# Transposing the last four tiles' attention weights on TensorE, other places for five weights, and one-column Newton steps in the norms

## The chip, the core and the metric

The kernel runs as one program on one core of a Trainium2 chip. Its time is the device time of one execution in microseconds (us); the figure given for a kernel is the median of several executions. The profile comes from one further execution, whose own time is given beside it. The engines are named as the profile names them: PE (TensorE's matmuls, with PEld for its weight loads), DVE (VectorE), ACT (ScalarE), POOL (GpSimd) and SP (SyncE, which here only issues DMA transfers).

## The reference: what is computed

Two layers of a small perceiver-like network on `x` of 32 x 64 x 256 (2048 tokens of 256 numbers), with a context of 32 x 256 x 256. All is float32. Each sublayer adds its result to `x`:

```
x += cross_attention_0(ctx, layernorm(x))    # 16 heads of 64; keys and values from ctx and from the latents
x += linear_attention(layernorm(x))          # 16 heads of 16, relu features
x += gated_ffn(layernorm(x))                 # hidden 768
x += cross_attention_1(layernorm(x), ctx)    # 16 heads of 16, a mask over the 256 keys
x += slstm(layernorm(x))                     # a scan over the 64 positions
x += moe(layernorm(x))                       # 8 experts 256 -> 1024 -> 256, gates by entmax over the 8 logits
```

What matters here is the second cross attention: for each batch item and head, `softmax(q k^T / 4 + mask)` over 256 keys, times `v`; and the layer norm, `(x - mean) / sqrt(var + eps)`.

## The kernel before

**Tiles.** The 2048 tokens are 16 tiles of 128 rows, and a tile holds two batch items. All 16 tiles of `x` stay in SBUF. Everything else lies in one large SBUF array, the arena, in which each named buffer has fixed places (`ar.put(phase, tag, size, *at)`, lines 693 to 756). Places of different phases may overlap; a buffer of a later phase may be written once all users of the overlapping earlier buffers are done. The big weights of the first cross attention are W0 (0 to 2048, the query weights), W1 (2048 to 4096, the transposed key weights), W2 (4096 to 6144, the value weights) and W3 (6144 to 8192). W0 and W1 are last read by the queries of the last group of items, W2 and W3 by the projection of the last tile. PSUM is handled as eight banks.

**Stages.** (1) The first cross attention, item by item (32 items). (2) Per group `g` of two tiles: linear attention, feed-forward, then for each tile the second cross attention, then the sLSTM and the router's logits. (3) The experts, part A for tiles 0 to 11 and part B for tiles 12 to 15, with gathers and scatters by indirect DMA on POOL's queue.

**Who sets the order.** The program is written as calls on `Plan`, which records operations with a `rank` (how early the author wants them) and a `lane` (PE operations of one lane stay in order). `Plan.run` (line 308) then simulates the engines with assumed durations (`PlanEngine.length`, line 519) and issues, again and again, the operation that can start first; an operation whose rank lies more than 12 above the lowest rank left waits (`pl.run(12.0)`, line 1959). For an `either` or a `copy` it picks ACT or DVE, whichever can start first. A transfer's end comes from one shared `wire` of 380 bytes per ns and a latency (lines 359 to 361). `Plan.locks` (line 370) keeps a DVE operation with three inner operands, such as `tensor_tensor` or `scalar_tensor_tensor`, from starting while a POOL operation runs in the plan, and the other way round; a `tensor_scalar` of fewer than 64 elements per row isn't kept so. What comes out is a fixed program: each engine runs its own list in order. All instructions of the plan therefore carry line 420 in the profile, and are told apart by the names of their tiles.

**The norms.** `ln_stats` (line 592) takes mean and variance of `n` tiles at once (n = 4 for the context, n = 2 elsewhere), forms `ve = var + eps`, lets POOL compute `r = ve ** -0.5`, and improves `r` by one Newton step in three DVE instructions on columns of `[128, n]` (lines 612 to 614). `normed` (line 1149) adds one for the shift `nmr = -mean * r`, and applies the norm on ACT or DVE. Both are called per group for `la`, `ff`, `xa`, `sl` and `me`; `lay` (the norm inside linear attention) uses the statistics alone, and so does `norm` (line 801) with a shift of its own for the first layer's `x` and context.

**The second cross attention.** `keys_values(t)` (line 1339) loads the tile's transposed context (`ctxT`), and makes keys (tiles `xak` in PSUM) with `x_wk` and values (`xav`) with `x_wv`. `scores(t, c, q, kT)` (line 1368) handles a block: one tile `t` and one half `c` of the heads, so 32 blocks in all. It computes the scores (`xsc`) into four banks, adds the mask and takes the maximum on DVE, and exponentiates on ACT into `pr`, for the tile's two items `b2`. The weights have then to be transposed so that keys lie on partitions. DVE's `transpose` does that only inside squares of 32 x 32, so that it takes two steps: one stream transpose of 128 x 1024 per item into `bT`, and then sixteen moves that shift pieces of 32 x 512 between partitions into `pT`:

```
for n in range(4):
    for a in range(4):
        k = (a + n) % 4
        move(n, pT[32 * k ...], bT[32 * a ...], tight=True)   # n == 1: a copy on ACT; else a DMA issued by SP
```

So a block has 4 copies on ACT and 12 DMA transfers of 64 KB on SP. `bT` and `pT` have one place each. `weighted` (line 1421) multiplies with `v` (`xpo`), scales by the sums (`xrT`), and `projected` (line 1448) adds the result to `x` (`xpw`).

**Loads.** The second layer's weights are loaded on SP's queue from line 1085 on: the feed-forward weights, then `x_wk`, `x_wv`, `x_wq`, `s_w`, the mask, `x_wo` in 16 pieces, `s_wp` and `m_wr`. Each of them goes out when its place is free. In the kernel before, `x_wk` and `x_wv` lie in W2 (4608 and 5120), `s_w` in W0 (1536), `s_wp` and `m_wr` in W1 (3584, 3840).

Of the kernel before, what the change touches and what calls it, by code (L numbers as in the profile page):

```python
# [9 lines left out]
F32 = mybir.dt.float32  # L10
I32 = mybir.dt.int32
AF = mybir.ActivationFunctionType
ALU = mybir.AluOpType
# [204 lines left out]
class Plan:  # L218
# [89 lines left out]
    def run(self, ahead):  # L308
        free = dict.fromkeys(self.ENGINES, 0.0)
        busy = dict.fromkeys(self.ENGINES, 0.0)  # L310
        wire = 0.0
        hold = {"DVE": (0.0, 0.0), "POOL": (0.0, 0.0)}
        calls_lock = self.locks
        ready = [op for op in self.ops if op.left == 0]
        todo = len(self.ops)
        waiting = set(self.ops)
        rest = sorted(self.ops, key=lambda op: -op.rank)
        while todo:
            best, short = None, None
            while rest[-1] not in waiting:  # L320
                rest.pop()
            for op in sorted(ready, key=lambda op: op.rank):
                if short is not None and op.rank > short.rank and "PE" in op.ways and op.news:
                    continue
                if op.rank > rest[-1].rank + ahead:
                    continue
                at = 0.0
                if op.news and not self.has_room(op):
                    if "PE" in op.ways and (short is None or op.rank < short.rank) and self.has_room(op, True):
                        short = op  # L330
                    continue
                since = self.since(op)
                for engine, (length, _) in op.ways.items():
                    at = max(free[engine], since)
                    for other in op.before:
                        at = max(at, other.done + (0.03 if other.on == engine else self.HOP))
                    for t_ in op.uses:
                        at = max(at, t_.free_at)
                    if engine in hold:
                        (lo, hi), other = hold[engine], calls_lock(op.ways[engine][1][0], engine)  # L340
                        if other and lo <= at < hi:
                            at = hi
                    key = at + (self.lean if engine == "DVE" and len(op.ways) > 1 else 0.0), op.rank
                    if best is None or key < best[0]:
                        best = key, op, engine
            assert best is not None, "nothing can start"
            (at, _), op, engine = best
            length, calls = op.ways[engine]
            todo -= 1
            ready.remove(op)  # L350
            waiting.remove(op)
            op.on = engine
            op.end = op.done = at + length
            free[engine] = op.end - self.OVERLAP.get(engine, 0.0)
            busy[engine] += length
            if engine in hold and self.locks(calls[0], engine):
                hold["POOL" if engine == "DVE" else "DVE"] = at, op.end
            if "dma" in calls[0][0]:
                size = PlanEngine.size_of(calls[0])
                wire = max(wire, op.end) + size / 380e3  # L360
                op.done = max(wire, op.end + size / 220e3) + (2.4 if engine == "POOL" else 1.5)
            self.issue(op, engine, calls)
            for other in op.after:
                other.left -= 1
                if other.left == 0:
                    ready.append(other)
        self.now, self.busy = max(op.done for op in self.ops), busy
# [178 lines left out]
def kernel(ctx: ExitStack, tc: tile.TileContext, d: dict, out: bass.AP):  # L546
# [45 lines left out]
    def ln_stats(srcs, name, lane="", twice=False, nc=nc, small=small):  # L592

        n = len(srcs)
        st = small.tile([P, n, 6], F32, tag=f"st{n}{lane}", name=f"st_{name}")
        mv = small.tile([P, n, 2], F32, tag=f"mv{n}{lane}", name=f"mv_{name}")
        for i, s_ in enumerate(srcs):  # L600
            nc.vector.bn_stats(st[:, i, :], s_)
            nc.vector.bn_aggr(mv[:, i, :], st[:, i, :])
        ve = small.tile([P, n], F32, tag=f"ve{n}{lane}", name=f"ve_{name}")
        if twice:
            nc.vector.tensor_scalar(ve, mv[:, :, 1], 1.0 + EPS, EPS * EPS, ALU.mult, ALU.add)
        else:
            nc.vector.tensor_scalar(ve, mv[:, :, 1], EPS, None, ALU.add)
        r = small.tile([P, n], F32, tag=f"r{n}{lane}", name=f"r_{name}")
        nc.gpsimd.tensor_tensor(r, ve, mhalf[:, 0:n], ALU.pow)

        t_ = small.tile([P, n], F32, tag=f"t{n}{lane}", name=f"t_{name}")
        nc.vector.tensor_tensor(t_, r, ve, ALU.mult)
        nc.vector.scalar_tensor_tensor(t_, t_, -0.5, r, ALU.mult, ALU.mult)
        nc.vector.scalar_tensor_tensor(r, t_, 1.5, r, ALU.add, ALU.mult)
        return mv, r


# [59 lines left out]
    with ExitStack() as sa:  # L677
# [31 lines left out]
        ar.put(1, "oT", 1024, 41472)  # L709

        for tag, size, *at in (
            ("f_wg", 1536, 0), ("s_w", 512, 1536), ("f_wu", 1536, 2048), ("s_wp", 256, 3584), ("m_wr", 16, 3840),
            ("x_wq", 512, 4096), ("x_wk", 512, 4608), ("x_wv", 512, 5120), ("x_wo", 512, 5632), ("f_wd", 1536, 6144),
            ("xTa", 512, 42496, 43008), ("qT", 512, 9728, 43520), ("xn0a", 256, 10240), ("xn1a", 256, 10496),
            ("lak", 256, 10752, 11008), ("kvb0", 272, 11264, 11536), ("kvb1", 272, 11808, 12080), ("y0", 256, 12352),
            ("lav", 258, 14336, 14594), ("y1", 256, 14852),
            ("xn0f", 256, 12800), ("xn1f", 256, 13056), ("xTf", 512, 13312, 13824),
            ("ffh", 1536, 17920), ("sg", 512, 20992, 21504),
            ("xn0x", 256, 16384), ("xn1x", 256, 16640), ("xTx", 512, 16896, 17408), ("xq", 1024, 32256, 33280),
            ("xcT", 1024, 22016, 19456), ("xkT", 1024, 23040, 24064), ("xv", 1024, 30208, 31232),  # L720
            ("xpr", 1024, 25088, 26112, 27136), ("xbT", 2048, 28160), ("xpT", 2048, 35328), ("xne", 256, 37376, 37632, 37888),
            ("xra", 256, 38144, 38400), ("xrT", 256, 38656, 38912), ("mi", 256, 39168), ("xom", 256, 39424, 39680),
            ("xoT", 256, 39936, 40192), ("mb", 256, 40448), ("vd", 256, 40704),
            ("xn0s", 256, 15360, 15616), ("xn1s", 256, 15872, 16128), ("xTs", 512, 34304, 34816),
            ("g_il", 260, 40960), ("g_m", 130, 7680), ("g_fs", 130, 7810), ("g_iz", 130, 7940), ("g_c", 130, 41220),
            ("hsel", 32, 41350), ("vb", 2, 41382), ("bo2", 1, 41384), ("hb", 4, 41386), ("g_z", 128, 12608), ("g_o", 128, 15108),
            ("g_tmp", 128, 41472), ("g_tmp2", 128, 41600), ("g_h", 128, 41728),
            ("a_wq", 512, 8192), ("a_wkv", 1024, 8704), ("rows_a", 1024, 44032),
        ):
            ar.put(2, tag, size, *at)  # L730
# [418 lines left out]
        def normed(srcs, name, lane, twice=False):  # L1149

            mv, r = stats(srcs, name, lane, twice)
            nmr = sp.tile([P, len(srcs)], F32, tag=f"nmr{lane}", name=f"nmr_{name}")
            pl.vector.scalar_tensor_tensor(nmr, mv[:, :, 0], -1.0, r, ALU.mult, ALU.mult)
            xn = []
            for i, s_ in enumerate(srcs):
                n_ = ar.tile([P, D], F32, tag=f"xn{i}{lane}", name=f"xn_{name}_{i}")
# [182 lines left out]
        def keys_values(t):  # L1339
# [25 lines left out]
                pl.copy(v[:, b2], pv)  # L1365
            return kT, v

        def scores(t, c, q, kT):


            pl.lane = "sc"
# [4 lines left out]
            with pl.together(1.45):  # L1376
                for b2 in range(2):
                    for j in range(4):
# [6 lines left out]
                            stop=True,  # L1385
                            tile_position=(32 * j, 0),
                        )
            bT = ar.tile([P, 4, 2, 2, 4, B_], F32, tag="xbT", name=f"xbT{nm}")
            for b2 in range(2):
                pr = ar.tile([P, 4, S2], F32, tag="xpr", name=f"xpr{nm}_{b2}")  # L1390
                for j in range(4):
# [1 line left out]
                    nmax = sp.tile([P, 1], F32, tag="xnm", name=f"xnm{nm}_{j}_{b2}")  # L1393
                    pl.vector.tensor_tensor_reduce(ne, scs[j][:, b2, :], mb, 1.0, 3.0e38, ALU.add, ALU.min, nmax)
                    pl.scalar.activation(pr[:, j, :], ne, AF.Exp, bias=nmax, scale=-1.0, accum_out=sm[:, b2, j : j + 1])
                pl.vector.transpose(
                    bT[:, :, b2].rearrange("p k d j c -> p j d k c"),
                    pr.rearrange("p j (d k c) -> p j d k c", d=2, c=B_),
                )
            pT = ar.tile([P, 4, 2, 2, 4, B_], F32, tag="xpT", name=f"xpT{nm}")  # L1400
            for n in range(4):
                for a in range(4):
                    k = (a + n) % 4
                    move(
                        n,
                        pT[B_ * k : B_ * k + B_, a].rearrange("p b d j c -> p (b d j c)"),
                        bT[B_ * a : B_ * a + B_, k].rearrange("p b d j c -> p (b d j c)"),
                        tight=True,
                    )
# [620 lines left out]
```

## Time and profile before

| what | us |
|---|---|
| three runs, median (lowest to highest) | 1606.68 (1605.44 to 1611.94) |
| the profiled execution's own time | 1614.4 |
| its span, first to last instruction | 1612.7 |
| PE busy, and its idle time between matmuls | 1513.3, some 80 |
| DVE, ACT, POOL busy | 1055.5, 830.6, 481.6 |

The mean granted clock of TensorE over the span is 0.976. The profile's page gives busy time by engine, then rows of 40 slices of 40 us in which a digit is the busy share in tenths. A line of a timeline reads: start, length, engine, operation, written tile <- read tiles, shape, count, and in brackets how long the engine stood idle before it and what released it. A line of a group gives total busy time, the mean in ns, and the idle time of the engine before them. The first layer fills the span to about 865 us, the groups of two tiles follow until about 1440, and the experts' matmuls run from 1376 to the last one at 1599.

### The profile page before, as it was taken

The numbers are of one execution on the slowest core, as the hardware profiler recorded it, in microseconds if no ns is written. First come the engines' busy times: TensorE is split into PE (matmuls) and PEld (weight loads), VectorE is DVE, ScalarE is ACT, GpSimd is POOL, SyncE is SP. The second block draws the span as 40 slices with busy tenths as digits, with TensorE's granted clock in tenths as the row PEclk, the third lists the DMA queues.
The fourth block names the chain that finished last, engine by engine and source line by source line (L and its number), as shares of the span: only waits on it lengthen the run. The fifth ranks groups of instructions, "written<-read, shape, count | busy, mean of one in ns | idle before, by whom it ended". The sixth has DMA issues, their size and how long they took to land. (4 is left out here: it accounts for less than half of the span.)

```text
span 1612.7 us, 25931 instructions
## 1 busy us (share of the span) xinstructions
PE 1513.3 (94%) x8594; PEld 1050.5 (65%) x8594; DVE 1055.5 (65%) x3119; ACT 830.6 (52%) x2193; POOL 481.6 (30%) x740
## 2 busy tenths in 40 slices
PE   7999999999999999999979999999999887899986
PEld 5565656566665656666546666667666665688875
DVE  7667566675665767766564787798897777553130
ACT  5555455454654546545431366666665576632332
POOL 6233224241242313432320122232232122233342
PEclk9999999999999999999999999999999997899998
DMA  5112212121111312123021032333333334655391
GB/s 178 33 33 57 46 26 58 23 60 34 36 40 37 76 30 40 30 73 89 17 60 49 25 78 71 80 85 73 78 88 91 100 85 121 181 151 144 76 301 31
DMA packets 114039, 120.21 MB, mean 75 GB/s; under 512 B 15472, under 2 KB 92081, under 8 KB 113905
## 3 DMA queue, kind: packets, MB, share of 16 engines
q1 hardware_dynamic: 108384, 110.60, 26.4%
q0 software_dynamic: 5520, 7.94, 2.5%
q8 instruction: 69, 1.13, 0.3%
q14 instruction: 66, 0.53, 0.1%
HBM read 63.63 MB, written 7.47 MB: 44 GB/s over the span
## 5 line engine op out<-in xcount | busy, mean ns | idle before, releaser
L420 PE MATMUL pu<-arena 128*128 128x512 f32 (+1 forms) x768 | 305.1, 615 | 7.4 <-DMA arena<-arena 7.4
L420 ACT COPY arena<-arena 32x128 f32<-32x128 f32 (+2 forms) x537 | 247.0, 460 | 118.2 <-DVE arena L420 59.0
L420 PE MATMUL sc<-arena 128*128 128x320 f32 x1024 | 293.0, 434 | 1.0 <-ACT arena L420 0.9
L420 POOL COPY arena<-arena 32x128 f32<-32x128 f32 (+2 forms) x285 | 138.5, 489 | 421.1 <-PE sc L420 264.7
L420 PEld LDWEIGHTS sc<-arena 128*128 128x128 f32 x1024 | 193.3, 190 | 102.3 <-issue 33.0
L420 ACT ACTIVATE arena<-sc,nmax 128x320 f32<-128x320 f32 x256 | 134.2, 526 | 224.0 <-DVE nmax L420 217.3
L420 DVE TENSOR_REDUCE nmax<-sc 128x1 f32<-128x320 f32 x256 | 122.6, 484 | 167.4 <-PE sc L420 164.9
L420 DVE STREAM_TRANSPOSE arena<-arena 128x256 f32<-128x256 f32 (+2 forms) x318 | 206.6, 688 | 26.4 <-POOL arena L420 16.0
L420 PEld LDWEIGHTS pu<-arena 128*128 128x128 f32 (+1 forms) x768 | 114.4, 189 | 158.1 <-issue 146.4
L420 POOL TENSOR_TENSOR arena<-arena 128x512 f32<-128x512 f32 (+2 forms) x157 | 145.3, 945 | 206.9 <-DVE arena L420 192.0
L420 ACT ACTIVATE arena<-arena,xnm 128x256 f32<-128x256 f32 x256 | 127.0, 497 | 41.5 <-DVE xnm L420 40.5
L420 DVE CUSTOM_DVE_ANT_0 arena<-xsc,arena 128x256 f32<-128x256 f32 x256 | 100.0, 417 | 8.2 <-ACT arena L420 6.2
L420 DVE TENSOR_TENSOR arena<-arena,sm 128x1280 f32<-128x1280 f32 x64 | 97.2, 1519 | 1.7
L420 POOL DMA_INDIRECT out<-arena x25 | 39.9, 1596 | 107.0 <-DVE arena L420 72.7
L420 PEld LDWEIGHTS po<-arena 128*64 128x64 f32 x1024 | 55.3, 137 | 21.2 <-issue 12.1
L420 PE MATMUL po<-arena 128*64 128x128 f32 x1024 | 62.7, 276 | 5.3 <-DVE arena L420 3.3
L420 PE MATMUL xav<-arena 128*128 128x256 f32 x256 | 63.1, 392 | 0.0
L420 DVE COPY arena<-pu 128x512 f32<-128x512 f32 x65 | 44.6, 687 | 27.4 <-PE pu L420 26.8
L420 PE MATMUL xak<-arena 128*128 128x512 f32 x128 | 62.3, 613 | 0.0
L420 PE MATMUL mepha<-arena 128*128 128x256 f32 x256 | 60.5, 388 | 0.7 <-ACT arena L420 0.7
L420 PE MATMUL pqk<-arena 64*128 64x256 f32 x512 | 61.1, 381 | 0.0
L420 PE MATMUL pq<-arena 128*128 128x256 f32 x256 | 57.3, 382 | 2.0 <-DVE arena L420 1.3
(396 smaller groups left out, 2510.5 us busy)
## 6 DMA issues: line engine op xcount, KB each, us to landing
arena<-in_m_w SPq DMA_DIRECT2D x26, 1024.0 KB
arena<-arena SPq DMA_DIRECT2D x384, 64.0 KB
arena<-arena SPq DMA_DIRECT2D x256, 80.0 KB
arena<-in_ctx SPq DMA_DIRECT2D x32, 256.0 KB
arena<-in_ctxT SPq DMA_DIRECT2D x16, 512.0 KB
x<-in_x SPq DMA_DIRECT2D x16, 128.0 KB
arena<-in_l0x_wkv SPq DMA_DIRECT2D x2, 1024.0 KB
arena<-arena SPq DMA_DIRECT2D x16, 128.0 KB
```

The source lines that it names most:

```text
L420: r = getattr(real, name)(*[get(a) for a in args], **{k: get(a) for k, a in kw.items()})
```

## The change

Four edits.

1. In `scores`, tiles 12 to 15 (`by_pe`) no longer use `bT` and the moves. Each item's weights are transposed by TensorE in two groups of four 128 x 128 transposes, each group into one PSUM bank, and each bank is copied by ACT or DVE into `pT`. Per block that is 16 transposes and 4 copies of 128 x 512 in place of 2 stream transposes, 4 ACT copies and 12 DMA transfers.
2. In the arena, `x_wk` moves to W0 (1536) and `x_wv` to W1 (3584); `s_w`, `s_wp` and `m_wr` move into W2 (4608, 5120, 5376).
3. In `ln_stats` with n <= 2, the three Newton instructions on both columns become two scalings of a single column by per-partition scalars, one instruction with two constants on both columns, and two more one-column scalings. In `normed`, the shift becomes one instruction per column. The sums are the same: `t = ve * r * r`, `t = 1.5 - t / 2`, `r = r * t`.
4. In the plan's simulation, the wire is kept per issuing engine and at 260 bytes per ns.

```diff
-        wire = 0.0
+        wire = dict.fromkeys(self.ENGINES, 0.0)
...
-                wire = max(wire, op.end) + size / 380e3
-                op.done = max(wire, op.end + size / 220e3) + (2.4 if engine == "POOL" else 1.5)
+                wire[engine] = max(wire[engine], op.end) + size / 260e3
+                op.done = max(wire[engine], op.end + size / 220e3) + (2.4 if engine == "POOL" else 1.5)
...
-        nc.vector.tensor_tensor(t_, r, ve, ALU.mult)
-        nc.vector.scalar_tensor_tensor(t_, t_, -0.5, r, ALU.mult, ALU.mult)
-        nc.vector.scalar_tensor_tensor(r, t_, 1.5, r, ALU.add, ALU.mult)
+        if n <= 2:
+            for i in range(n):
+                nc.vector.tensor_scalar(t_[:, i : i + 1], ve[:, i : i + 1], r[:, i : i + 1], r[:, i : i + 1], ALU.mult, ALU.mult)
+            nc.vector.tensor_scalar(t_, t_, -0.5, 1.5, ALU.mult, ALU.add)
+            for i in range(n):
+                nc.vector.tensor_scalar(r[:, i : i + 1], r[:, i : i + 1], t_[:, i : i + 1], None, ALU.mult)
+        else:
...
-            ("f_wg", 1536, 0), ("s_w", 512, 1536), ("f_wu", 1536, 2048), ("s_wp", 256, 3584), ("m_wr", 16, 3840),
-            ("x_wq", 512, 4096), ("x_wk", 512, 4608), ("x_wv", 512, 5120), ("x_wo", 512, 5632), ("f_wd", 1536, 6144),
+            ("f_wg", 1536, 0), ("x_wk", 512, 1536), ("f_wu", 1536, 2048), ("x_wv", 512, 3584),
+            ("x_wq", 512, 4096), ("s_w", 512, 4608), ("s_wp", 256, 5120), ("m_wr", 16, 5376), ("x_wo", 512, 5632), ("f_wd", 1536, 6144),
...
-            pl.vector.scalar_tensor_tensor(nmr, mv[:, :, 0], -1.0, r, ALU.mult, ALU.mult)
+            for i in range(len(srcs)):
+                pl.vector.tensor_scalar(nmr[:, i : i + 1], mv[:, i, 0:1], r[:, i : i + 1], -1.0, ALU.mult, ALU.mult)
...
+        def by_pe(t, c):
+            return t >= 12
...
+                if by_pe(t, c):
+                    pl.lane = "tp"
+                    if b2 == 0:
+                        pT = ar.tile([P, 4, 2, 2, 4, B_], F32, tag="xpT", name=f"xpT{nm}")
+                    for kc in range(2):
+                        pT_ps = bank([P, 4, P], f"xpTp{nm}_{b2}_{kc}")
+                        with pl.together(T4):
+                            for j in range(4):
+                                tr(pT_ps[:, j, :], pr[:, j, kc * P : (kc + 1) * P], ident)
+                        pl.copy(
+                            pT[:, :, b2, kc].rearrange("p a j c -> p j a c"),
+                            pT_ps.rearrange("p j (a c) -> p j a c", a=4),
+                        )
+                else:
+                    pl.vector.transpose(...)
...
-            for n in range(4):
+            for n in range(0 if by_pe(t, c) else 4):
```

More of the change, by code (lines that the diff above doesn't have):

```diff
@@ L611, in ln_stats @@
         t_ = small.tile([P, n], F32, tag=f"t{n}{lane}", name=f"t_{name}")
-        nc.vector.tensor_tensor(t_, r, ve, ALU.mult)
-        nc.vector.scalar_tensor_tensor(t_, t_, -0.5, r, ALU.mult, ALU.mult)
-        nc.vector.scalar_tensor_tensor(r, t_, 1.5, r, ALU.add, ALU.mult)
+        if n <= 2:
[5 more added lines that the diff above has]
+        else:
+            nc.vector.tensor_tensor(t_, r, ve, ALU.mult)
+            nc.vector.scalar_tensor_tensor(t_, t_, -0.5, r, ALU.mult, ALU.mult)
+            nc.vector.scalar_tensor_tensor(r, t_, 1.5, r, ALU.add, ALU.mult)
         return mv, r
@@ L1387, in scores @@
                         )
-            bT = ar.tile([P, 4, 2, 2, 4, B_], F32, tag="xbT", name=f"xbT{nm}")
+            if not by_pe(t, c):
+                bT = ar.tile([P, 4, 2, 2, 4, B_], F32, tag="xbT", name=f"xbT{nm}")
             for b2 in range(2):
@@ L1395, in scores @@
                     pl.scalar.activation(pr[:, j, :], ne, AF.Exp, bias=nmax, scale=-1.0, accum_out=sm[:, b2, j : j + 1])
[L1396 to L1400, printed above, removed]
-            for n in range(4):
+                if by_pe(t, c):
[12 more added lines that the diff above has]
+                else:
+                    pl.vector.transpose(
+                        bT[:, :, b2].rearrange("p k d j c -> p j d k c"),
+                        pr.rearrange("p j (d k c) -> p j d k c", d=2, c=B_),
+                    )
+            if not by_pe(t, c):
+                pT = ar.tile([P, 4, 2, 2, 4, B_], F32, tag="xpT", name=f"xpT{nm}")
+            for n in range(0 if by_pe(t, c) else 4):
                 for a in range(4):
```

## The prediction

> **What bounds the kernel.** I read the page first, then busy time by stage, then the timelines of TensorE and of the SP queue, because the chain of waits ends on the last indirect write and holds nothing else (two pieces, 1.3 us).
>
> ```profile
> PE 1513.3 (94%) x8594; PEld 1050.5 (65%) x8594; DVE 1055.5 (65%) x3119; ACT 830.6 (52%) x2193; POOL 481.6 (30%) x740
> ...
> PE   7999999999999999999979999999999887899986
> ...
> PEclk9999999999999999999999999999999997899998
> ```
>
> TensorE is busy nearly everywhere; its row dips in two places, at the slices around 840 us and from 1300 us on, and the second dip is also where the granted clock falls. The same by stage (us, then busy us of PE, PEld, DVE, ACT, POOL, then the clock):
>
> ```profile
> 780.00:880.00 100.00, 87.27 (x413) 54.09 (x412) 52.20 (x128) 30.89 (x73) 16.44 (x35) 0.93 0.21 51
> 880.00:1220.00 340.00, 323.61 (x2327) 232.52 (x2325) 281.09 (x997) 202.74 (x554) 86.91 (x164) 0.99 0.28 71
> 1220.00:1410.00 190.00, 161.07 (x1202) 121.14 (x1203) 137.35 (x508) 118.86 (x324) 46.38 (x82) 0.90 0.43 118
> 1410.00:1600.00 190.00, 183.29 (x1058) 159.94 (x1056) 62.37 (x310) 60.16 (x152) 68.80 (x62) 0.98 0.53 149
> ```
>
> What can be won: 12.7 us of TensorE idle at the change of layers, 16.4 in the steady second layer (95% busy), 28.9 in its tail, 6.7 among the experts. In the tail a clock of 0.90 means 38 us at half speed (0.10 x 190 / 0.5), of which TensorE worked 161/190, 32 us, so up to 16 us more. Everything else is TensorE work, and the change adds to that.
>
> **Part 1, the weights' places.** The timeline of TensorE at the change of layers:
>
> ```profile
> 839.80 1.49 PE L420 MATMUL lac<-arena 128*64 128x136 f32 x8 [3.35 <-DVE arena L420]
> 846.12 5.22 PE L420 MATMUL pu<-arena 128*128 128x512 f32 x8 [4.83 <-DMA arena<-arena]
> ...
> 892.13 3.70 PE L420 MATMUL xak<-arena 128*128 128x512 f32 x8
> 895.67 1.89 PE L420 MATMUL xav<-arena 128*128 128x256 f32 x8
> 897.40 0.60 PE L420 MATMUL tr_xa<-ident,arena 128*128 128x128 f32 x4
> 897.83 1.89 PE L420 MATMUL xav<-arena 128*128 128x256 f32 x8
> ```
>
> TensorE stands 3.35 + 4.83 = 8.2 us while the last item's probabilities are transposed and moved, and has nothing else it may do. Keys and values of tile 0 (xak, xav) have their context already (the two ctxT loads issue at 823.01), but not their weights:
>
> ```profile
> 741.12 0.49 SPq L420 DMA_DIRECT2D arena<-in_f_wu  x1
> ...
> 864.64 0.38 SPq L420 DMA_DIRECT2D arena<-in_x_wk  x1
> ...
> 1383.63 9.23 SPq L420 DMA_DIRECT2D arena<-arena  x12
> ```
>
> x_wk and x_wv lie in W2 and wait for its last reader, the projection that ends at 865; in W0 and W1 they can load by 741, as f_wu does. So xak (892.13 to 895.67, 3.5 us) and two xav groups (1.7 each, 3.5) can fall into the hole: their ranks are 40.9 to 42.1, and the planner, which lets a step run 12 ahead of the lowest rank left, allows 41.8 to 43 while item 31's last steps (29.8 to 31) stand. The output of xak lies over score operands that the last scores (834) free; that of xav over a buffer that the last stream transpose (839.6) frees, so xak fits the first gap and xav the second. The copies go to ACT, busy 2.2 of these 10 us. **Bounds: nothing** (planned elsewhere) **to 10.5 us** (both gaps, and half of the 4.6 us worked at half clock there). I take **-7.0**, tile 0's keys and values. The two loads pass 1.4 us of SP issue ahead of the context loads of tile 15 at 742.7, which are wanted tens of us later; s_w, s_wp and m_wr move behind 865, next to x_wo, and are first read over 100 us later. Cost nothing.
>
> **Part 2, the norms.** 56 statistics of two columns go from 3 DVE instructions to 5, and 40 shifts from 1 to 2: 56 x 2 + 40 = 152 more. An undisturbed chain now starts its steps 0.2 us apart (t_ff at 853.52, 853.71, 853.90, nmr at 854.10): 0.8 us. The nearest new form is the pair of 128x2 scalings by a column at 860.57: 0.35 us for two, 0.39 with the same hand-over of 0.04. Three pairs and one plain step are 3 x 0.39 + 0.20 = 1.37, so +0.57 a chain, and without the shift +0.38: 40 x 0.57 + 16 x 0.38 = 29 us of DVE. What goes:
>
> ```profile
> L420 DVE TENSOR_TENSOR t_me<-r_me,ve_me x8: 109/679/683, 999.8 to 1436.1; 128x2 f32<-128x2 f32 x8
> ```
>
> The same instruction takes 0.11 or 0.68 us (minimum, median, maximum); 14 of these two-column steps took over 0.5, some 0.5 too long each: 7 us. No one-column TENSOR_SCALAR in the trace took over 0.22. The Trainium skill ("SBUF — State Buffer", Who interferes with whom) explains it: a DVE instruction with two SBUF inputs is blocked by a GpSimd one that reads SBUF, one with a single input outside the two-port modes is not. By that rule the 7 us go wholly; the same section lets tensor_scalar enter a two-port mode, which speaks against the remaining two-column step. DVE net: from -7 (stalls gone, steps free) to +22 us. DVE has room (281 of 340 us), so only what sits in front of a TensorE wait counts: **+2.0**, a tenth of 22; the range keeps -7 and +10, nearly half.
>
> **Part 3, tiles 12 to 15.** Per block (a tile's half; 8 blocks), from the groups:
>
> ```profile
> L420 DVE STREAM_TRANSPOSE arena<-arena 128x1024 f32<-128x1024 f32 x64 | 78.8, 1238 | 9.0 <-ACT arena L420 6.7 <-DMA arena<-arena 1.9 <-DMA out<-x 0.2
> L420 ACT COPY arena<-arena 32x512 f32<-32x512 f32 x128 | 78.8, 616 | 34.0 <-DVE arena L420 20.0 <-remote 5.4 <-DVE xsm L420 5.2
> ```
>
> Away: 16 stream transposes, 19.8 us of DVE; 32 ACT copies, 19.7; 96 moves on SP at 0.62 us (7.48 for twelve at 1354.85) or more, 60 us. Added: 32 copies of 128x512 out of PSUM, 0.58 on ACT or 0.69 on DVE (the pu copies), 18.6 to 22 us on either; so the two engines together win about 19. Added on TensorE: 32 groups of four transposes; tr_xa above occupies it 0.43 (897.40 to 897.83), tr_me 0.44 and tr_ff 0.49 elsewhere: 32 x 0.45 = **+14.4**, with no cover, since TensorE is the bound.
>
> What it buys is latency. The last two blocks' stream transposes end at 1383.4 and 1396.8, their twelve moves are issued in 9.23 us from 1383.63 (the SP lines above) and 10.98 from 1400.23, and their xpo start at 1395.78 and 1414.94: 12 and 18 us. Four transposes and a copy are 0.45 + 0.6, so that path becomes some 3 us, and in the tail, with no next group to fill in, TensorE gets ready work earlier.
>
> ```profile
> 1349.83 1.94 PE L420 MATMUL xpo<-arena 128*32 128x128 f32 x32
> ```
>
> Of the 28.9 us idle, 7.1 are xpo of tiles 10 and 11 waiting for their moves (1233, 1251, 1268), which stay; 2.7 wait for a gather and 1.6 for router steps. Of the other 17.5 (3.7 before gT_psA at 1341.8 and 3.6 before slp at 1374.1 among them) I take two thirds as filled: -11.7. Half clock follows the gaps; the line above shows its price, 1.94 us where the other blocks' xpo take 1.08. Three stretches of 3.4 us behind gaps that stay keep 10 of the 32 us; the other 22 cost 11, of which I take five sixths, -9.2. Sum: 14.4 - 11.7 - 9.2 = **-6.5**. Bounds: +14.4 (no gap closes) to -22: the stage's work, 145 us at full clock (190 - 28.9 - 16) plus 14.4, at the steady 95% is 168 of 190.
>
> New waits: the transposes wait for four exponentials (0.69 us each with their read), their copies for the previous block's xpo; behind them on TensorE stand whatever was planned next and, in PSUM, four more of eight banks while the scores hold four.
>
> A rule that speaks against this part is in the Trainium skill ("TensorE: Matmul & The Clock Gate", PE-mode transpose): transposes do not count as TensorE work for the clock. No row here isolates it. With one extra window of 3.4 us (same page) at half clock per block, the estimate would be 8 x 1.7 = 14 us more, a loss in place of the gain.
>
> **Part 4, the planner's wire.** 260 in place of 380 bytes/ns, and one wire per issuing engine: no instruction changes, the order may. TensorE waits for DMA in all about 25 us (xpo 10.0, pu 7.4, tr_xga 2.7, wkTp 2.2, pvb 1.9, last 0.9). I take 0, with 5 either way.
>
> **Sum.** -7.0 + 2.0 - 6.5 = -11.5. The profiled execution took 1614.4 us (span 1612.7, and 1.7 around it), giving 1602.9. It ran 7.7 above the median of 1606.68, to which the forecast refers: 1595.2, **1595 us**.
>
> **Rivals.** (a) Forecast, 0.50, own range 1586 to 1602. (b) TensorE pays, slower, 0.18: the tail's gaps stay, as the waits that end last are the sLSTM chain, the router and the moves of tiles 10 and 11; +14.4 + 2, and half the weights' gain lost behind other work (-3.5): 1606.7 + 12.9 = 1620. It decides once part 3 recovers less than 14.4 + 2 - 7 = 9.4 us of the 45 there (28.9 idle, 16 of clock). For it: no xpo of tiles 12 to 15 is itself late by its moves. Against: the clock falls to 0.64 in that stage. (c) Nothing nets, 0.17: the hole at 840 is filled by work that was no bound later (DVE, 83% busy, paces the second layer) and the tail breaks even, 1606. (d) The tail closes to the steady 95%, -22, the hole -10, order and norms 0: 1575, 0.15. For it: ACT and DVE lose 19 us and SP 60.
>
> A measurement tells 0.5%, 8 us, from no change. Faster by more (below 1598.6): three quarters of (a), all of (d), a little of (c), 0.55. Within: 0.29. Slower (above 1614.7): most of (b) and a little of (c), 0.16. The range takes in (d) and (b): 1577 to 1620.
>
> **What would show it.** Right: xak before 850 and no gap near 4.8 us before pu; TENSOR_SCALAR steps near 0.2 with none at 0.68; xpo of tiles 12 to 15 within 5 us of their last exponential; the clock at 0.95 or more over the tail. Wrong: xak still near 890; TensorE idle in the tail above 18 us; more DVE-ended idle in 880 to 1220.

## The result

The changed kernel took 1616.89 us (median of 16 runs) where the kernel before took 1609.45 in the same series: a ratio of 1.0044, 95% interval 1.0030 to 1.0058. It is slower by about 7 us (0.0044 x 1606.68); the forecast was 11.5 faster. The prediction gave 0.29 to a time within 8 us of before, and the 7 us lie there, on the slow side; with 16 runs of each kernel they are clear of the noise.

### The profile page after: what moved, and what is told of

It is laid out like the page before. It is cut to its first block, busy times and chain, and to the rows that moved or that the text cites. A ratio compares the mean times of both kernels' runs of the same rounds, so it can differ in the third digit from the quotient of the medians.

```text
span 1615.2 us, 26197 instructions
## 1 busy us (share of the span) xinstructions
PE 1522.4 (94%) x8722; PEld 1056.2 (65%) x8722; DVE 1064.3 (66%) x3253; ACT 829.3 (51%) x2195; POOL 483.4 (30%) x740
## 3 DMA queue, kind: packets, MB, share of 16 engines
q1 hardware_dynamic: 103776, 104.31, 24.5%
## 5 line engine op out<-in xcount | busy, mean ns | idle before, releaser
L420 ACT COPY arena<-arena 32x128 f32<-32x128 f32 (+2 forms) x509 | 228.5, 449 | 90.9 <-DVE arena L420 45.6
L420 DVE STREAM_TRANSPOSE arena<-arena 128x256 f32<-128x256 f32 (+2 forms) x302 | 187.0, 659 | 20.9 <-POOL arena L420 14.1
L420 PEld LDWEIGHTS po<-arena 128*64 128x64 f32 x1024 | 55.3, 137 | 20.1 <-issue 11.7
L420 PE MATMUL pq<-arena 128*128 128x256 f32 x256 | 62.6, 404 | 1.3 <-ACT arena L420 1.3
## 6 DMA issues: line engine op xcount, KB each, us to landing
arena<-in_ctx SPq DMA_DIRECT2D x32, 256.0 KB
```

Of the source, the lines that this page charges most:

```text
L420: r = getattr(real, name)(*[get(a) for a in args], **{k: get(a) for k, a in kw.items()})
```

## The profile after

The profiled execution took 1616.92 us, its span 1615.2. Busy time by engine, TensorE's row by slices, and the granted clock:

```profile
PE 1522.4 (94%) x8722; PEld 1056.2 (65%) x8722; DVE 1064.3 (66%) x3253; ACT 829.3 (51%) x2195; POOL 483.4 (30%) x740
...
PE   7899999999999999999999989999999998999996
...
PEclk9999999999999999999999999999999999999998
```

Both dips that the prediction showed are gone, at 840 us and from 1300 us on, and the clock is full nearly throughout. Two slices fell from 9 to 8, at 40 to 81 and at 929 to 969 us; beyond that these rows don't say why the kernel isn't faster. The table by stage says more (us; PE, PEld, DVE, ACT, POOL busy; clock):

```profile
780.00:880.00 100.00, 96.30 (x439) 56.92 (x439) 56.83 (x140) 35.86 (x86) 18.32 (x36) 0.98 0.20 48
880.00:1220.00 340.00, 313.98 (x2285) 228.09 (x2284) 290.14 (x1062) 205.02 (x554) 86.90 (x164) 0.98 0.27 69
1220.00:1410.00 190.00, 173.22 (x1434) 129.51 (x1432) 144.89 (x586) 110.67 (x318) 50.70 (x90) 1.00 0.32 92
1410.00:1600.00 190.00, 180.21 (x982) 157.56 (x983) 53.90 (x285) 59.73 (x148) 64.20 (x53) 0.96 0.51 147
```

The idle time of TensorE fell from 12.7 to 3.7 us in the first row and from 28.9 to 16.8 in the third, and rose from 16.4 to 26.0 in the second, where DVE's busy time rose from 281 to 290: the steady second layer got worse. In the fourth row it rose from 6.7 to 9.8. TensorE at the change of layers:

```profile
840.88 1.13 PE L420 MATMUL pu<-arena 64*128 64x512 f32 x4
841.84 0.61 PE L420 MATMUL lakvs<-arena 64*128 64x129 f32 x8
842.38 0.68 PE L420 MATMUL lac<-arena 128*64 128x136 f32 x8
842.99 3.70 PE L420 MATMUL xak<-arena 128*128 128x512 f32 x8
846.62 0.79 PE L420 MATMUL lac<-arena 128*64 128x136 f32 x8
847.34 3.72 PE L420 MATMUL xav<-arena 128*128 128x256 f32 x16
```

Keys (xak) and values (xav) of tile 0 now run here, 49 us earlier, with no bracketed gap. Steps of the norms of the feed-forward (ff) and of the experts (me), with minimum, median and maximum in ns; the first line is from the kernel before:

```profile
L420 DVE TENSOR_TENSOR t_ff<-r_ff,ve_ff x8: 149/156/683, 853.5 to 1267.8; 128x2 f32<-128x2 f32 x8
...
L420 DVE TENSOR_SCALAR t_ff<-ve_ff,r_ff x16: 261/265/272, 857.1 to 1270.9; 128x1 f32<-128x1 f32 x16
L420 DVE TENSOR_SCALAR r_ff<-r_ff,t_ff x16: 200/205/215, 858.3 to 1271.5; 128x1 f32<-128x1 f32 x16
L420 DVE TENSOR_SCALAR t_ff<-t_ff x8: 155/406/684, 857.6 to 1271.2; 128x2 f32<-128x2 f32 x8
...
L420 DVE TENSOR_SCALAR t_me<-t_me x8: 169/194/200, 998.8 to 1410.4; 128x2 f32<-128x2 f32 x8
```

One instruction on one column takes 0.205 us, or 0.265 with two column scalars; in the kernel before, one instruction on both columns took 0.156 at the median. Most of the long cases went, not all. Before, 14 two-column steps took over 0.3 us, together 6.9 us more than at 0.16 each; now 7 do, with 2.1 us. Six of the 7 are the one step that still works on two columns (t_ff five times, t_xa once, only one of them over 0.5 us); the seventh, a shift in the first layer, is one that the change leaves alone. One `var + eps` step has become long beside them (0.629 us). For the experts' norm, where the step shown in the prediction had a median of 0.679, none is above 0.274.

The last two blocks' transposes, weighted sums and projection:

```profile
1374.98 1.97 PE L420 MATMUL xpTp<-ident,arena 128*128 128x128 f32 x16
1377.53 1.08 PE L420 MATMUL xpo<-arena 128*32 128x128 f32 x32
1379.51 1.04 PE L420 MATMUL xpTp<-ident,arena 128*128 128x128 f32 x8
1381.25 1.04 PE L420 MATMUL xpTp<-ident,arena 128*128 128x128 f32 x8
1382.95 1.08 PE L420 MATMUL xpo<-arena 128*32 128x128 f32 x32
1385.79 1.03 PE L420 MATMUL xpw<-arena 128*128 128x256 f32 x4
```

The last exponential ends at 1381.4, xpo starts 1.6 us later, and the last projection starts at 1385.8 (1419.5 before). Over the eight blocks of tiles 12 to 15 the distance is 1.6 to 5.0 us, where it was 11.5 to 21.5.

So three of the four signs of a right forecast came; the fourth, steps without a long case, did not come in full. Of the signs of a wrong one, one came: the idle time of TensorE that DVE ended between 880 and 1220 us, in the twelve largest groups of waits, is 9.7 us, 7.0 before. This rise of 2.7 is less than a third of the 9.6 us by which TensorE's idle time grew there; xpo waiting for ACT, in none of these groups before, has 6.6. The experiments ask which edit costs, and how.

## Experiments: the four edits apart

Each kernel is compared with the kernel before in the same series on the same chip. A difference in us is (ratio - 1) x 1606.68. "In place" means that the plan is computed with the old steps, so that every engine's order is unchanged, and other instructions are issued where the old ones stood:

```diff
-        for name, args, kw in calls:
+        for name, args, kw in getattr(op, "instead", calls):
```

**e1_wire** has only edit 4, the two lines of the wire.

> The kernel before with the planner's wire alone changed (per engine, 260 bytes per ns); no instruction is added or removed, only the order may differ. Theory N (the norms' one-column steps cost the second layer its 14 us): the wire does little, between -3 and +5 us, and what it costs lies in the first 110 us, where the changed kernel lost 6 us. Theory W (the new order of the whole plan costs it): +10 to +20 us, with the second layer's group of two tiles at 63 us in place of 61.

Measured: 1.0076 (1.0047 to 1.0105), +12 us. In the profile the steady first layer (from the end of the first tile's po, the first half of its projection, to the second layer's first queries) takes 694.0 us, against 690.1 in a second profile of before (e12); the other kernels with the new wire have 694.1 (e7) and 694.3 (the changed one), all those without it 690.1 to 690.5. The first items are issued in another order, and 4 us are not won back. Where the rest lies, the profiles don't show; theirs differ by 5 us only. The 12 us fit theory W, but not its sign: the second layer's groups take as long as before (sixteen blocks from the fifth 248.5 us, 248.2 in e12).

**e2_places** has only edit 2.

> The kernel before with the places of five weights alone changed. Both theories: xak of tile 0 starts near 840 us in place of 892 and the hole of 8.2 us closes, -7 to -14 us (14 is what the changed kernel won between the start of the second layer's linear attention and its first scores). A rival, that the hole is filled and the time given back in the second layer because DVE paces it: -3 to +3 us, with the group of two tiles longer than 61 us.

Measured: 0.9967 (0.9947 to 0.9988), -5.3 us. From the second layer's first queries to its first scores 116.3 us in place of 129.4 (131.5 in e12), but the next four blocks 60.3 in place of 54.5 (55.8): some 13 to 15 won at the hole, 5 given back behind it. The result lies between the two ranges.

**e3_norms** has only edit 3, planned anew.

> The kernel before with the norms' steps alone changed (one-column scalings in the Newton step and the shift). Theory N: +8 to +16 us, most of it between 900 and 1230 us, DVE busy time of the norms' steps 40 to 82 us. Theory W: 0 to +4 us.

Measured: 1.0123 (1.0093 to 1.0153), +20 us, above the range of theory N and far above W's. The sixteen blocks from the fifth take 256.0 us in place of 248.0.

**e4_by_pe** has only edit 1.

> The kernel before with tiles 12 to 15 transposed by TensorE alone changed. If the tail's gain is what the traces of before and after show between the scores of tile 10 and the last matmul (382 against 378 us): -2 to -8 us, with the last tile's cross attention done some 30 us earlier and the experts' end moved far less, since TensorE has 14 us more to do. A rival, that the transposes' 14 us are not recovered without the other edits: +3 to +14 us.

Measured: 0.9991 (0.9967 to 1.0015), no difference. The stage from tile 12's first scores to the last projection (the tail in what follows; the expectation of e12 says the last group's scores) falls from 147.0 (e12) to 108.4 us, and the stage from there to the last matmul grows from 171.6 to 205.1: the work of TensorE is moved, not removed.

**e5_norms_in_place** issues the new steps in the unchanged order:

```diff
         nc.vector.scalar_tensor_tensor(r, t_, 1.5, r, ALU.add, ALU.mult)
+        if n <= 2:
+            col = lambda v, i: v[:, i : i + 1]
+            nc.ops[-3].instead = [("tensor_scalar", (col(t_, i), col(ve, i), col(r, i), col(r, i), ALU.mult, ALU.mult), {}) for i in range(n)]
+            nc.ops[-2].instead = [("tensor_scalar", (t_, t_, -0.5, 1.5, ALU.mult, ALU.add), {})]
+            nc.ops[-1].instead = [("tensor_scalar", (col(r, i), col(r, i), col(t_, i), None, ALU.mult), {}) for i in range(n)]
...
```

> The plan of the kernel before, instruction for instruction and in its order, but where it issues the norms' Newton steps and shifts, the new one-column instructions are issued in their place; so the steps' own cost without a new order. The one-column edit alone, planned anew, cost 20 us. If the steps themselves cost it (DVE busy time for them 40 to 81 us in either case, a chain of 1.28 in place of 0.75 us): +12 to +20 us. If the new order that the plan makes of them costs it: 0 to +6 us.

The shift is replaced likewise.

Measured: 1.0097 (1.0073 to 1.0120), +15.6 us. The instructions themselves cost most of it, not a new order. The same stage of sixteen blocks takes 257.0 us. TensorE's idle time that DVE ended between 880 and 1220 us, 7.1 us in e12, is 14.0; the group that grew most, in e12 and then here (total, times, longest, in us):

```profile
PE tr_la L420 <- DVE ve_ff L420: 1.6, 3, 0.5
...
PE tr_la L420 <- DVE ve_ff L420: 5.5, 4, 1.6
```

**e6_places_by_pe** has edits 1 and 2; **e7_all_but_norms** 1, 2 and 4; **e8_all_but_wire** 1, 2 and 3.

> The two edits that did not lose, together: the weights' places and the transposes by TensorE, with the norms and the wire of before. If the parts add: -5.3 and -1.4, so -7 us, between -3 and -12; this would be faster than both kernels. If what the places win is given back in the second layer and the transposes need the late end of the tail to pay: -3 to +3 us.

> The changed kernel without the norms' edit (places, transposes by TensorE and wire stay). The norms' edit is the cause of the loss if this is 12 to 20 us below the changed kernel, that is -4 to -13 us against the kernel before. If the parts only add up by chance of the order, it stays within 3 us of the kernel before.

> The changed kernel with the planner's wire of before. If the wire's order costs what its run alone showed, this is some 10 us below the changed kernel, -3 us against before, with the first layer's steady part 4 us shorter (690 in place of 694 us). If the wire only hurt with the old moves in the tail, it is as the changed kernel, +5 to +9 us, and only those 4 us of the first layer go.

Measured: e6 0.9953 (0.9934 to 0.9973), -7.6 us; e7 0.9995 (0.9979 to 1.0010), -0.8; e8 1.0047 (1.0027 to 1.0066), +7.6. The norms cost 15 us on top of e6, and 8 (1.0044 against 0.9995) on top of e7. The wire costs 7 on top of e6 and nothing on top of e8. So these two edits do not add, and why is not shown; without them the other two make a kernel faster than both. By its own expectation e7 speaks against the norms as the only cause: it is 8 us below the changed kernel, not 12 to 20, and within 3 us of before. e8 shows that taking out the wire alone changes nothing: only without both are 7.6 us won.

## Experiments: how the norms cost

The new steps add 20.9 us to DVE's busy time (1076.5 in e5, 1055.6 in e12) and cost 15.6, although DVE has some 60 of 340 us idle in that part of the kernel. Three theories: the chain got longer in front of TensorE (latency); DVE's list is full (occupancy); the instructions are dear for another reason. The next kernels leave all old steps and add 192 scalings of a constant column into a spare one, in unchanged order, at three places. The lines below are those of e9; in e10 and e13 the same stands behind `pl.vector.transpose` in `scores` and behind the gate `(sg + 1) * pg` of the feed-forward:

```diff
+    spare = const.tile([P, 4], F32, tag="spare", name="spare")
...
             pl.vector.scalar_tensor_tensor(nmr, mv[:, :, 0], -1.0, r, ALU.mult, ALU.mult)
+            pl.ops[-1].instead = [("tensor_scalar", (spare[:, i : i + 1], mhalf[:, i : i + 1], mhalf[:, i : i + 1], None, ALU.mult), {}) for i in range(4)] + pl.ops[-1].ways["DVE"][1]
```

**e9_in_chain**: four ahead of the last step of each of 48 norms.

> The kernel before, with four one-column scalings of a constant added ahead of the last DVE step of each norm of the second layer (the shift, or r for lay): 192 instructions, 0.205 us each by the changed kernel's one-column steps, so 39 us of DVE and 0.82 us in each of 48 chains; plan and order unchanged. The results are not changed. In the unchanged order the new steps added 42 us of DVE and cost 14 us. Latency (a norm's steps stand before TensorE's next work, and DVE time costs only there) and occupancy (DVE paces the second layer, and DVE time costs anywhere) both say +10 to +16 here. If neither holds, and the new steps cost for some reason of their own (their form, or what they wait for), this stays under +5.

Measured: 1.0074 (1.0047 to 1.0101), +11.9 us; the sixteen blocks 256.9.

**e10_in_cover**: three ahead of each stream transpose.

> The same 192 one-column scalings, three ahead of each of the 64 stream transposes of the second cross attention, where DVE stands some 1 us for the last exponential (20 us in 21 waits between 940 and 1210 us): 0.62 us of DVE each time, 39 us in all; plan and order unchanged, results unchanged. Latency says 0 to +4: the time lies in a wait that was there. Occupancy says +10 to +16, as with the same instructions in the norms.

Measured: 1.0101 (1.0069 to 1.0134), +16.2 us; the sixteen blocks 258.0. Latency in the norms is out: no norm is longer here. The delay of the transposes' own chain (exponential, transposes, moves, xpo) is not told apart from that of DVE's list. But the place was not the one that was meant. The 20 us that the expectation speaks of were all waits of DVE for ACT, and few of them stand ahead of stream transposes. The groups of e12, with the idle time before them behind the bar:

```profile
L420 DVE STREAM_TRANSPOSE arena<-arena 128x1024 f32<-128x1024 f32 x64 | 78.8, 1237 | 7.2 <-ACT arena L420 6.0 <-DMA arena<-arena 0.7 <-issue 0.2
L420 DVE SCALAR_TENSOR_TENSOR arena<-arena,ffg 128x512 f32<-128x512 f32 x24 | 16.4, 684 | 27.9 <-ACT arena L420 27.9
```

The transposes have 7.2 us ahead of them, the 24 gates of the feed-forward 27.9. In e10:

```profile
L420 DVE STREAM_TRANSPOSE arena<-arena 128x1024 f32<-128x1024 f32 x64 | 79.1, 1235 | 2.4 <-ACT arena L420 1.0 <-DMA arena<-arena 0.9 <-issue 0.5
L420 DVE TENSOR_SCALAR spare<-mhalf 128x1 f32<-128x1 f32 x192 | 28.4, 203 | 0.0
L420 DVE SCALAR_TENSOR_TENSOR arena<-arena,ffg 128x512 f32<-128x512 f32 x24 | 16.4, 683 | 27.1 <-ACT arena L420 26.9
```

The scalings took 28.4 us, of which the waits they stood in gave 4.8; the gates wait as long as before, because what they wait for (TensorE's product, then ACT's tanh) came later by as much. DVE's 83% is not 17% to spare: its idle time lies in a few places, and work put elsewhere doesn't reach it.

**e11_no_newton**: the other direction; the kernel leaves out the Newton step of the two-column norms.

```diff
+        if n <= 2:
+            for op in nc.ops[-3:]:
+                op.instead = []
```

> The kernel before with the three DVE instructions of the Newton step left out of the 56 norms of two columns (r is then POOL's power alone), plan and order unchanged: some 0.55 us less in each chain, 31 us of DVE. If DVE time in the norms costs a third of itself, as the new steps did, this gives it back the other way: -8 to -13. If the path switches, so that the next wait (POOL's power, a transfer) is late at once, -4 to 0.

Measured: 0.9970 (0.9951 to 0.9990), -4.8 us for 23.1 us of DVE (1032.5 in place of 1055.6): under the expected 8, over the 4 of the path that switches. The sixteen blocks take 244.0 us. Taking DVE time away gains less per us than adding it costs.

**e12_before_again**: a second profile of before.

> The kernel before, unchanged, for a second profile: the first one was 7.7 us above the median, and where its excess lies bears on every comparison by stages. Expected 1604, the tail (last group's scores to the last projection) shorter than 145.5 us, and the steady part of the second layer (16 blocks from the fifth) 248 again.

Measured: 1610.28 us, the sixteen blocks 248.2, and the tail 147.0 us, not shorter than 145.5. What the first profile had in excess lay among the experts (178.3 us from the last projection to the last matmul, against 171.6).

**e13_in_waits**: twelve ahead of each of 16 gates, where DVE does wait.

> The kernel before with the same 192 one-column scalings, now twelve ahead of each of 16 gates of the feed-forward (the first two of each group's three), where DVE stood longest: 1.4 to 3.0 us before 13 of the 16 in the second profile of before, waiting for the tanh; 12 x 0.14 us of issue is 1.7 us each, 27 us in all. Plan, order and results unchanged. If DVE's list is what paces the second layer, and only its waits are free, -1 to +4, and the stage of 16 blocks stays near 248 us. If the instructions cost for another reason than the time they take from DVE (their reads, their number), +10 again.

```diff
+                if f2 < 2:
+                    pl.ops[-1].instead = [("tensor_scalar", (spare[:, i % 4 : i % 4 + 1], mhalf[:, i : i + 1], mhalf[:, i : i + 1], None, ALU.mult), {}) for i in range(12)] + pl.ops[-1].ways["DVE"][1]
```

Measured: 0.9999 (0.9981 to 1.0018), nothing; the sixteen blocks 249.5 us. Its groups:

```profile
L420 DVE TENSOR_SCALAR spare<-mhalf 128x1 f32<-128x1 f32 x192 | 24.5, 203 | 0.0
...
L420 DVE SCALAR_TENSOR_TENSOR arena<-arena,ffg 128x512 f32<-128x512 f32 x24 | 16.4, 684 | 6.5 <-ACT arena L420 6.2
```

The wait ahead of the gates fell from 27.9 to 6.5 us: it took in 21.4 of the 24.5. In the busy time, DVE 1077.1 us here against 1075.8 in e10 and 1076.5 in e5, the three kernels are alike; one costs nothing and two cost 16 us. So the price isn't in the instructions. It is the place in DVE's list: ahead of a wait it is free, elsewhere it delays what follows. The sixteen blocks say the same: against 209.8 us busy and 38.4 idle in e12, DVE has 220.5 and 37.5 in e10, where the stage grew, and 222.8 and 26.7 here, where the idle time shrank instead.

**e14_places_by_pe_pool**: e6, with the Newton step on POOL.

```diff
+        v_ = nc.gpsimd if n <= 2 else nc.vector
+        v_.tensor_tensor(t_, r, ve, ALU.mult)
+        if n <= 2:
+            v_.tensor_tensor(t_, t_, r, ALU.mult)
+            v_.tensor_scalar(t_, t_, -0.5, 1.5, ALU.mult, ALU.add)
+            v_.tensor_tensor(r, r, t_, ALU.mult)
...
-                return 0.7 if n <= 2 else 1.0
+                return 0.2 if ALU.pow not in args else 0.7 if n <= 2 else 1.0
```

> The weights' places and the transposes on TensorE, without the wire and the new norm steps, and with the Newton step of the 56 norms of two columns on POOL, as four operations after its power, planned at 0.2 us each. That takes 168 small instructions, some 23 us, off DVE and lengthens each chain by POOL's time for four. If DVE's list paces the second layer, this is below the 1596 of the same kernel with DVE's Newton step: 1589 to 1594. If POOL's operations are long (0.3 us or more) or the changed order costs, 1596 to 1606.

Measured: 0.9916 (0.9891 to 0.9941), -13.5 us, the fastest kernel of the study. Its steady second layer from 960 to 1210 us, and then e6's DVE and its own by the page:

```profile
960.00:1210.00 250.00, 239.04 (x1830) 172.38 (x1829) 202.99 (x690) 158.81 (x436) 85.69 (x231) 1.00 0.32 81
```

```profile
PE 1511.3 (95%) x8722; PEld 1051.9 (66%) x8722; DVE 1043.5 (66%) x3120; ACT 819.7 (52%) x2176; POOL 480.8 (30%) x740
```

```profile
PE 1518.2 (95%) x8722; PEld 1055.6 (66%) x8722; DVE 1012.4 (63%) x2949; ACT 819.8 (51%) x2179; POOL 521.3 (33%) x964
```

DVE gave up 31 us and POOL took 40; TensorE is busy 239.0 of 250 us, against 236.5 in e12. Against e6 (0.9953) the ratio is some 6 us lower, as expected, but the two ran in different series and their intervals touch: that it beats both kernels is shown, that POOL's Newton step alone is worth 6 us is not.

## Why the prediction was wrong

**The step that failed is part 2, the norms**: "DVE has room (281 of 340 us), so only what sits in front of a TensorE wait counts: +2.0, a tenth of 22." The durations were about right: an undisturbed chain takes 1.28 us where 1.37 was worked out (0.75 before), and DVE's net was 20.9 us, inside -7 to +22. The share that counts was wrong: 15.6 of 20.9, three quarters, not a tenth; inside the whole change the norms still cost 8 us (e7), where +2.0 was forecast. A mean busy share was read as room. e10 and e13 show what stood in its place: the same 20 us or so of DVE time cost 16 us in a full stretch of its list and nothing ahead of an instruction that waits. It was the mechanism of rival (c), "DVE, 83% busy, paces the second layer", which the prediction used against the weights' gain and not against the norms' cost. The range's end of +10 for the norms was too low as well. The norms are the largest miss, not the only one: without their edit the change is worth -0.8 us (e7), and the rest up to the forecast lies in parts 3 and 4.

Of the 7 us of long steps, expected to go wholly, some 5 went. The two-column step that stays is still held, at up to 0.684 us, and of the one-column ones none is above 0.274. In both traces a POOL instruction ran beside each long step, which ended 0.01 to 0.03 us after it. This is how the Trainium skill ("SBUF — State Buffer", Who interferes with whom) has it, in the clause that the prediction named as speaking against this step: `tensor_scalar` can enter a two-port mode and then contends with GpSimd.

**Part 1, the weights, was right.** -7.0 forecast, -5.3 measured alone (0.9967). xak and xav went where the prediction put them. The gain at the hole was larger than forecast, 13 us, and part of it was given back in the next group, which is rival (c)'s doubt in part.

**Part 3, the transposes, was right in its mechanism and nearly in each term, but not in the sum.** Alone against e12, over the tail and the experts together: idle time of TensorE fell from 24.7 to 14.4 us, 10.3 in place of 11.7. Work at half clock fell from 26.8 to 9.2 us, which is worth 8.8 in place of 9.2. The added work is larger: 128 transposes take 17.5 us busy in the changed kernel, 0.55 a group of four, not 0.45 as for tr_xa. 17.5 - 10.3 - 8.8 = -1.6; -1.4 was measured, which the noise doesn't tell from zero (0.9967 to 1.0015), and -6.5 was forecast. That the sum meets the runs so closely is luck: in the two profiles tail and experts together are 5.1 us shorter. A small difference of large terms deserved bounds of its own. Rival (b), that the tail's gaps stay, is refuted; its 1620 lies nearer to the measured time than the forecast does, for another reason. The clock over the tail is 1.00 with 128 transposes in it, so the estimate of 14 us of extra half-clock time did not come about; it was worked out from the Trainium skill ("TensorE: Matmul & The Clock Gate", PE-mode transpose), whose rule that transposes don't count as work no run here isolates, since other matmuls stand between them.

**Part 4, the wire, was not nothing.** Alone it costs 12 us, more than the 5 either way that the part allowed, with edits 1 and 2 some 7, with all three nothing. 4 us lie in the first layer's order, and the changed kernel has them too. Where the rest lies, and why the cost vanishes in company, stays open.

**The sum.** The edits alone, -5.3, -1.4, +20 and +12, would make +25; the whole change measured +7. The plan's order depends on all four at once, so that single effects need not add; those of edits 1 and 2 do (-6.7 added, -7.6 measured). By stages of the two profiles, the changed kernel against e12: 6.7 us more up to the second layer's first queries, 16.0 less from there to its first scores, 8.2 more in the next four blocks and 9.6 more in the twenty after them, 1.8 less in tail and experts together, in all 6.7 more. What was won at the change of layers was given back in the second layer.

## What to carry to other kernels

An engine's idle share is room only where it waits: before costing added work at nothing, look up which instruction of that engine stands behind its idle time, and whether the new work comes directly ahead of it. If not, expect to pay for most of its busy time (here two thirds to four fifths), at least where the engine's waits, as here for ACT, move with its own work. Splitting a small instruction over its columns multiplies its fixed cost; a quieter engine at the same point of the chain (here POOL, which had already made the power) may be the better place, though its worth by itself wasn't shown here.

## What the runs showed of the hardware

- Width hardly mattered for DVE's small `tensor_scalar` steps: by one column scalar, one column took 0.205 us in the changed kernel, two columns 0.22 and eight 0.22 to 0.23. With two column scalars one column took 0.265, with constants alone two columns 0.17 where nothing held them.
- Of DVE's two-column steps, 14 took 0.52 to 0.68 us in the kernel before, each beside a POOL instruction and ending 0.01 to 0.02 us after it.
- POOL's four steps on 128 x 2 took 0.19 to 0.23 us in the mean of each group, where its power took 0.70 to 0.87:

```profile
L420 POOL TENSOR_TENSOR r_ff<-ve_ff,mhalf 128x2 f32<-128x2 f32 x8 | 5.7, 716 | 5.0 <-DVE ve_ff L420 5.0
...
L420 POOL TENSOR_TENSOR t_ff<-r_ff,ve_ff 128x2 f32<-128x2 f32 x8 | 1.6, 196 | 0.2
```

- A lone group of four transposes of 128 x 128 float32 on TensorE took 0.60 us, eight in a row 1.04 to 1.09 and sixteen 1.97; the granted clock stayed at 1.00 over the stage from 1220 to 1410 us that holds all 128.
